# Moving splits, sums, a bias and a branch in a two-part graph network kernel

## The chip, the cores and the metric

The kernel runs on one core of a Trainium2 chip. A core has a matrix engine (TensorE, PE in the profile; its weight loads are listed as PEld), VectorE (DVE), ScalarE (ACT), GpSimd (POOL) and SyncE (SP), which here only issues transfers. Each engine works through its own queue of instructions in order and meets the others by semaphores. SBUF is the on-chip memory, PSUM the accumulators that TensorE writes, and DRAM is reached by DMA.

The metric is the device time of one execution in microseconds (us).

## The reference, cut to what matters

There are 1250 nodes with 1024 features, and 20000 edges sorted by their target. Two graph networks run one after the other, all in float32, each followed by a residual and a layer normalisation.

```
# first network
h = layernorm(x) * g + b
h = relu(h @ W1 + b1) @ W2 + b2              # 1024 -> 512 -> 256
for i in range(3):
    z = h + segment_sum(h[src], dst)
    z = relu(z @ Wa[i] + ba[i]) @ Wb[i] + bb[i]
    h = h + relu(layernorm(z) * ng[i] + nb[i])
delta = relu(h @ Wd1 + bd1) @ Wd2 + bd2      # 256 -> 512 -> 1024
x = layernorm(x + layernorm(x + delta) * og + ob)
# second network, two layers
deg_inv = 1 / max(in_degree, 1)
for l in range(2):
    mean = segment_sum(h[src], dst) * deg_inv
    h = h @ Wself[l] + mean @ Wneigh[l] + b[l]   # relu after the first
out = layernorm(x + h)
```

## The kernel before, in words

Every float32 product is made of three products of rounded halves: each operand is split into `hi` (rounded by ScalarE, `split_w` L123) and `lo = raw - hi` (a subtraction on VectorE or GpSimd), and `mm3` (L112) adds hi*hi, hi*lo and lo*hi in PSUM. So each weight costs one ScalarE pass and one subtraction.

**Encoder (0 to about 122 us).** Node rows are handled in tiles of 128 (ten tiles, pairs in `PCH`). A first block (L232 to L273) and a second (L502 to L554) are written in a fixed order by hand (`manual_schedule` over DVE, ACT, POOL and PE). They check the edge list, normalise and transpose the first x tiles, split W1 and run the first chunk of x @ W1. VectorE derives codes from the edge list in three steps (`codes(0..2)`, L278) that the one-hot matrices need.

The edges are summed into a dense adjacency matrix `A` (nodes by nodes, resident in SBUF). For each group of five edge tiles VectorE builds one-hot matrices R and Q (`one_hots`, L329), TensorE multiplies them into PSUM (`edge_tile`, L351), ScalarE copies a window of 50 columns into A at a place read from the integers `anci`, and GpSimd adds a carried column. This runs in between the encoder's products (`y_chunk`, `h_rows`), chunks 1 to 4.

The window scheme only works for edge lists that are dense enough. The first block counts whether this holds and leaves an integer `fli`: 0 for the fast way, 1 for the general one. `flag` (L389) is loaded from it on every engine, and `any_edges` (L390) holds a branch, `tc.If(flag > 0)`, around `general_adjacency`. It stands at the start of chunk 1. A second branch (L578) after the last edges reads A back. With these inputs neither body is entered; each engine has to compare and jump. `anci` is limited from above on VectorE (L264), so that the window stays inside A also for lists that take the general way.

After the last edges the unit matrix is added to A's diagonal (L577), so that A @ h is h + agg.

**Layers (about 122 to 262 us).** `load_wab(i)` (L611) loads and splits Wa[i] and Wb[i]; `begin_layer(i)` (L625) loads the layer's vectors. `agg(i, c, ..)` (L640) multiplies h by a block of A's columns and splits the result into `zh`, `zl`; `z1_chunk` (L657) and `z2_rows` (L670) are the two dense products, the normalisation and the new h rows. `asum` is the sum of A over its ten row blocks; the in-degrees come from it in `degrees` (L597, in layer 1). Rows 0 to 5 are summed ahead of the first `agg` (L744 to L746); rows 6 to 9 stand in layer 0's loop (L782 to L784) in two half widths. In the loop with i = 0, A is written to DRAM (`A_d`, L781), and W of layer 2 and the first two row blocks of the decoder's Wd2 are loaded; the third comes in layer 1 (L765). The branch for i = 1 (L789 to L791) loads Wd1, the last block of Wd2 and, by `load_bdo` (L710), the decoder's bias: four broadcast loads, six subtractions on VectorE and eight ScalarE passes, for three bfloat16 parts of bd2 - ob.

Layer weights, Wd1 and Wd2 are subtracted on GpSimd (`eng=G` in L611, `G` in L699 and L708). All of these loads, the layer's `bb` and the bias go through one ring of three buffers (`wraw`, L120), which also serves the second network. SP issues them in order; a load waits until the buffer's last user is done.

**Decoder and second network (262 us to the end).** The decoder's products, the second network with its seven half-size products per layer, and the output rows. The change touches nothing here.

Outside the hand-written blocks a planner in the framework fixes each engine's order when the program is built. It goes by the order in the source as priority, and by estimated durations and dependences: work that is late in the source can be put early in an engine's queue if the planner thinks the engine free, and a branch is one unit to it, with nothing of its body mixed with what is outside. On the chip the order is fixed.

Of the kernel before, what the change touches and what calls it, by code (L numbers as in the profile page):

```python
# [62 lines left out]

@with_exitstack
def tile_gnn(ctx, tc, x, es, vecs, W1, W2, b2, Wa, Wb, bb, ng, nb, Wd1, Wd2, bd2, og, ob,
             Ws0, Wn0, b0l, Ws1, Wn1, b1l, out):
# [101 lines left out]
    est = S1.tile([P, 2 * NGR * GT + 3 * (NGR + 1) + 3 * GT], I32, name="est")  # L168
    ne, o = NGR * GT, 2 * NGR * GT
    esrc, edst = est[:, :ne], est[:, ne:o].rearrange("p (g j) -> p g j", j=GT)  # L170
    anc, atop, agap = (est[:, o + i * (NGR + 1):o + (i + 1) * (NGR + 1)] for i in range(3))
    o += 3 * (NGR + 1)
# [59 lines left out]
    with tc.high_priority(), tc.manual_schedule(engines=order):  # L232
# [31 lines left out]
        V.tensor_tensor(anci, anc[0:1], atop[0:1], ALU.min)  # L264
# [6 lines left out]
        fli = S1.tile([1, 1], I32, name="fli")  # L271
        V.tensor_copy(fli, flf)
# [101 lines left out]
    def ahead(g):  # L374
        nonlocal n_oh
        while n_oh < min(NGR, g):
            one_hots(n_oh)
            n_oh += 1

    def some_edges(k):  # L380
        nonlocal n_ed
        for _ in range(k):
            ahead(n_ed // GT + LOOK + 1)
            if n_ed < ET:
                edge_tile(n_ed)
                n_ed += 1


    flag = nc.values_load(fli[0:1, 0:1], min_val=0, max_val=1)  # L389
    def any_edges():  # L390

        with tc.If(flag > 0):
            acc = Ap.tile([P, NT, AW], F32, name="acc", tag="A")
            V.memset(acc, 0.0)
            scratch = [B1.tile([P, 8 * (PW + 2)], F32, name=f"g{s}", tag=f"h0{s}0", bufs=1) for s in "hl"] + spare
            general_adjacency(tc, psp, acc[:, :, :N], (esrc, est[:, ne:2 * ne]), ident, ones, x, A_g, xg_d, scratch)
            res = Ap.tile([P, NT, AW], F32R, name="A", tag="A")
            nc.sync.dma_start(res.bitcast(F32)[:, :, :NN], A_g)
        return res
# [102 lines left out]
    with tc.manual_schedule(engines=order):  # L502
        std0 = bn_std(bn_mv(st0, 0))
        mv1 = bn_mv(bn(1), 1)

        parts = [bn_norm(0, *std0, ((0, HEAD), (HEAD, D)))]
        next(parts[0])
        parts.append(bn_norm(1, *bn_std(mv1), ((0, HEAD), (HEAD, D))))
        next(parts[1])
        split_W1(0, V)  # L510
        for part in parts:
            next(part)

        h0[0] = new_h0(0)
        for j in range(2):
            S.activation(h0[0][0][:, :, PW + j], vec[:, C_B:C_B + 8], AF.Copy)
            V.tensor_sub(h0[0][1][:, :, PW + j], vec[:, C_B:C_B + 8], h0[0][0][:, :, PW + j].bitcast(F32))
        transpose_x(0, (0,))
        split_W1(1)
        warm_up(WC)  # L520
        transpose_x(0, (2,))
        split_W1(2)
        mv2 = bn_mv(bn(2), 2)
        split_W1(3)
        std2 = bn_std(mv2)
        split_W1(4)
        next(bn_norm(2, *std2))
        codes(0)
        for f in range(4):
            first[f] = pst("ps_y", "ps" if f < 2 else "pa")  # L530
        for k in range(8):
            for f in range(4):
                fs = slice(f * P, f * P + P)
                mm3(first[f][:, :PW + 2], W1h[:, k, fs], W1l[:, k, fs], h0[0][0][:, k], h0[0][1][:, k],
                    k == 0, k == 7)
            if k == 0:
                transpose_x(0, (4,))
                split_W1(5)
                codes(1)
                mv3 = bn_mv(bn(3), 3)  # L540
            if k == 2:
                transpose_x(0, (6,))
                split_W1(6)
                std3 = bn_std(mv3)
                split_W1(7)
                next(bn_norm(3, *std3))
                codes(2)
            if k == 6:
                transpose_x(1, (0,))
        transpose_x(1, (2,))  # L550
        transpose_x(1, (4, 6))
        load_W2()
        V.tensor_copy(onesr, ones)
        ahead(2)  # L554
    for f in range(4):
        V.tensor_add(b1c[:, f:f + 1], first[f][:, PW:PW + 1], vec[:, C_B1 + f:C_B1 + f + 1])
    NC = len(PCH)
    SLOTS = 13
    for c in range(NC):
        if c == 1:  # L560
            A = any_edges()
        for f in range(4):
# [10 lines left out]
            if slot == SLOTS - 1:  # L573
# [4 lines left out]
                with tc.If(flag > 0):  # L578
                    nc.sync.dma_start(A.bitcast(F32)[:, :, :NN], A_g)
# [31 lines left out]
    def load_wab(i, eng=G):  # L611
# [81 lines left out]
    def load_Wd1():  # L693
        wd1h, wd1l = (B2.tile([P, 2, DH], F32R, name=f"wd1{s}", tag=f"w1{s}") for s in "hl")
        wd1.extend((wd1h, wd1l))
        for k in range(2):
            raw = wraw()
            nc.sync.dma_start(raw, Wd1[k * P:(k + 1) * P])
            split_w(raw, wd1h[:, k], wd1l[:, k], G)  # L699

    def load_Wd2(k):
        both = WD2.tile([P, 2, D], F32R, name=f"wd2_{k}", tag=f"wd2_{k}")
        hi, lo = wd2[k] = both[:, 0], both[:, 1]
        for i in range(2):
# [3 lines left out]
            split_w(raw, hi[:, fs], lo[:, fs], G)  # L708
# [35 lines left out]
    V.tensor_add(asum, A[:, 0, :NN].bitcast(F32), A[:, 1, :NN].bitcast(F32))  # L744
    for t in range(2, 6):
        V.tensor_add(asum[:gz(t)], asum[:gz(t)], A[:gz(t), t, :NN].bitcast(F32))  # L746
# [3 lines left out]
    for i in range(3):  # L750
# [12 lines left out]
        if i == 1:  # L763
            degrees()
            load_Wd2(2)  # L765
# [13 lines left out]
        if i == 0:  # L779
            with tc.issue_after(loads["nb"].ins):  # L780
                nc.sync.dma_start(A_d, A.bitcast(F32)[:, :, :NN])  # L781
            for t in range(6, NT):  # L782
                for cs in (slice(0, NN // 2), slice(NN // 2, NN)):
                    V.tensor_add(asum[:gz(t), cs], asum[:gz(t), cs], A[:gz(t), t, cs].bitcast(F32))  # L784
            load_wab(2)
            for k in range(2):
                load_Wd2(k)
        else:
            load_Wd1()  # L789
            load_Wd2(3)  # L790
            load_bdo()  # L791
# [877 lines left out]
```

## Time and profile before

| | |
|---|---|
| median of three runs | 923.88 us (922.95 to 924.91) |
| the profiled execution | 923.78 us, span 921.9 us |
| busy: PE, PEld | 894.7 us (97%), 788.2 us (85%) |
| busy: DVE, ACT, POOL | 645.0, 394.2, 87.7 us |
| mean granted TensorE clock | 0.99 |
| HBM read, written | 103.35 MB, 49.21 MB |

The span runs from the first to the last instruction; the device time is 1.9 us longer. Busy times overlap. A line such as `40.30 0.55 PE L113 MATMUL ps_h<-w2h,yh ... [4.00 <-PEq L392]` says: at 40.30 us TensorE began an instruction of line 113 that took 0.55 us, after 4.00 us idle that ended with its own sequencer at line 392. Line 113 to 115 are `mm3`, so tiles tell such lines apart. `PEclk` is the share of TensorE's full clock that was granted. Instructions of a queue's sequencer (`PEq`, `SPq`) do not count as busy time.

### The profile page before, as it was taken

To read this page: it belongs to the slowest core of one execution; us is meant where nothing else is said; L and a number is where in the kernel's file an instruction comes from. 1 tells how busy PE (TensorE), PEld (TensorE's weight loads), DVE (VectorE), ACT (ScalarE), POOL (GpSimd) and SP (SyncE) were. 2 spreads that over 40 slices of the span, in tenths; PEclk is the share of its full clock that TensorE was granted. 3 is DMA by queue.
4 is the path that set the end of the run, shared out by engine and by line. 5 is a ranking of instruction groups with operands and counts; after the bars stand their busy time and mean duration, and the time that the engine had idled before them with its cause. 6 is when DMAs were issued, how large, how long until landed. Compare 5 with 4: busy or idle time off the path is not lost.

```text
span 921.9 us, 13248 instructions
## 1 busy us (share of the span) xinstructions
PE 894.7 (97%) x4777; PEld 788.2 (85%) x4783; DVE 645.0 (70%) x1311; ACT 394.2 (43%) x760; POOL 87.7 (10%) x122
## 2 busy tenths in 40 slices
PE   7799998999899999999999999999999999999997
PEld 6799998988887778999988888889999888888885
DVE  8799678595976775565677675547466786777785
ACT  4577523454566873211133354543111333333454
POOL 4022234344201000000000000000000000000000
PEclk9799999999999999999999999999999999999999
DMA  7310058953115649997442236537895722322214
GB/s 243 118 42 2 1 197 217 312 177 103 61 52 202 224 145 348 336 310 254 170 148 72 77 127 197 172 125 264 287 306 214 235 80 77 85 72 76 81 47 177
DMA packets 83666, 148.35 MB, mean 161 GB/s; under 512 B 8296, under 2 KB 31995, under 8 KB 83082
## 3 DMA queue, kind: packets, MB, share of 16 engines
q1 hardware_dynamic: 77206, 126.90, 41.4%
q0 software_dynamic: 2176, 10.27, 4.5%
q10 hardware_dynamic: 4212, 10.27, 3.0%
q8 instruction: 38, 0.62, 0.3%
q14 instruction: 34, 0.28, 0.1%
HBM read 103.35 MB, written 49.21 MB: 165 GB/s over the span
## 4 chain that ended last, share of the span: by engine, by line
PE 83%; DVE 6%; DMA 4%; ACT 1%; issue 1%; POOL 0%; ACTq 0%; DVEq 0%; POOLq 0%; SPq 0%
PE ps_A L1222 20%; PE ps_m L113 14%; PE ps_m L115 14%; PE ps_m L114 14%; DMA wraw<-in_Wd_dram 3%; PE ps_dd L113 2%; PE ps_dd L115 2%; PE ps_dd L114 2%; PE pa L358 2%; PE ps_y L113 2%; PE ps_y L114 1%; PE ps_y L115 1%; PE ps_z L649 1%; DVE asum L746 1%; PE pt L974 1%
## 5 line engine op out<-in xcount | busy, mean ns | idle before, releaser
L113 PE MATMUL ps_m<-w,th 128*128 128x512 f32 x520 | 204.1, 392 | 0.0
L115 PE MATMUL ps_m<-w,th 128*128 128x512 f32 x520 | 202.6, 390 | 0.0
L114 PE MATMUL ps_m<-w,th 128*128 128x512 f32 x520 | 202.3, 389 | 0.0
L1222 PE MATMUL ps_A<-A,qh 128*128 128x418 f32 (+1 forms) x480 | 170.5, 355 | 0.0
L1222 PE MATMUL ps_A<-A,ql 128*128 128x418 f32 (+1 forms) x480 | 169.9, 354 | 0.0
L115 PEld LDWEIGHTS ps_m<-w,th 128*128 128x128 f32 x520 | 97.6, 188 | 20.7
L113 PEld LDWEIGHTS ps_m<-w,th 128*128 128x128 f32 x520 | 97.6, 188 | 19.8
L114 PEld LDWEIGHTS ps_m<-w,th 128*128 128x128 f32 x520 | 97.7, 188 | 19.7
L125 DVE TENSOR_TENSOR w<-stage,w 128x512 fp32r<-128x512 f32 x65 | 44.7, 690 | 68.2 <-ACT w L124 67.9
L1222 PEld LDWEIGHTS ps_A<-A,ql 128*128 128x128 f32 (+1 forms) x480 | 90.8, 189 | 1.9
L124 ACT ACTIVATE w<-stage 128x512 fp32r<-128x512 f32 x65 | 40.7, 629 | 118.8 <-PE ps_m L115 76.7
L1222 PEld LDWEIGHTS ps_A<-A,qh 128*128 128x128 f32 (+1 forms) x480 | 90.3, 188 | 1.2
L1227 DVE TENSOR_TENSOR MT<-ps_A,dgb 128x418 f32<-128x418 f32 x48 | 25.5, 586 | 64.6 <-PE ps_A L1222 64.6
L1183 ACT ACTIVATE qh<-qraw 128x1280 fp32r<-128x1280 f32 (+3 forms) x28 | 21.5, 809 | 105.1 <-PE ps_A L1222 102.8
L113 PE MATMUL ps_y<-h0h,w1h 128*128 128x256 f32 (+2 forms) x160 | 52.9, 331 | 0.0
L125 DVE TENSOR_TENSOR w<-wraw,w 128x512 fp32r<-128x512 f32 x39 | 26.9, 689 | 32.5 <-ACT w L124 30.7
L114 PE MATMUL ps_y<-h0l,w1h 128*128 128x256 f32 (+2 forms) x160 | 46.3, 289 | 2.9 <-DVE h0l L450 2.9
L1311 DVE TENSOR_TENSOR c<-ps_m,c 128x512 f32<-128x512 f32 (+1 forms) x65 | 40.9, 682 | 8.8 <-PE ps_m L115 8.7
L115 PE MATMUL ps_y<-h0h,w1l 128*128 128x256 f32 (+2 forms) x160 | 45.9, 287 | 0.0
L1052 ACT ACTIVATE th<-XT 128x640 fp32r<-128x640 f32 x48 | 34.2, 724 | 20.5 <-DVE MT L1227 20.5
L124 ACT ACTIVATE w<-wraw 128x512 fp32r<-128x512 f32 x39 | 24.5, 628 | 41.6 <-PE ps_m L115 21.3
L1053 DVE TENSOR_TENSOR th<-XT,th 128x640 fp32r<-128x640 f32 x48 | 39.5, 822 | 0.0
(307 smaller groups left out, 1842.4 us busy)
## 6 DMA issues: line engine op xcount, KB each, us to landing
A<-A_d SPq DMA_DIRECT2D x20, 627.0 KB
w_d<-stage SPq DMA_DIRECT2D x43, 256.0 KB
stage<-w_d SPq DMA_DIRECT2D x43, 256.0 KB
stage<-in_l_W_neigh_dram SPq DMA_DIRECT2D x42, 256.0 KB
stage<-in_l_W_self_dram SPq DMA_DIRECT2D x28, 256.0 KB
A_d<-A SPq DMA_DIRECT2D x1, 6270.0 KB
wraw<-in_l_W_neigh_dram SPq DMA_DIRECT2D x22, 256.0 KB
w_d<-wraw SPq DMA_DIRECT2D x21, 256.0 KB
```

Of the source, the lines that this page charges most:

```text
L113: T.matmul(ps, a_hi, b_hi, start=start, stop=False, skip_group_check=go_on)
L114: T.matmul(ps, a_hi, b_lo, start=False, stop=False, skip_group_check=go_on)
L115: T.matmul(ps, a_lo, b_hi, start=False, stop=stop, skip_group_check=go_on)
L124: S.activation(hi, raw, AF.Copy)
L125: return eng.tensor_sub(lo, raw, hi.bitcast(F32))
L358: T.matmul(pa[g][:, :, lo:hi], R[:, j], Q[j], start=j == 0, stop=end, skip_group_check=True)
L1052: S.activation(hi, src, AF.Copy)
L1053: V.tensor_sub(lo, src, hi.bitcast(F32))
L1183: S.activation(q[0][:, t0:t1], raw[:, t0:t1], AF.Copy)
L1222: T.matmul(pss[j][c][:, :w], qs[j][s][:n, t], A_of(t)[:n, c0:c0 + w], start=start and s == 0, stop=stop and s == 1)
L1227: V.tensor_mul(MT[:, f, c0:c0 + w], pss[j][c][:, :w], dgb[:, c0:c0 + w])
L1311: V.tensor_add(c, ps[:n], c if last or M in (6, 7) else c11[:n, t])
```

## The change

- The program body is now a function `gnn(..., fli, general, ...)` that is called twice: first the fast way, unconditionally; then `fli` is loaded and a branch holds a whole second copy, which computes everything again the general way. The two branches in the encoder and the flag's load there are gone. The copy without the general way has no `general_adjacency`.
- So that the fast copy stays inside A for every list, `anci` is now chosen between the true bases and even ones (a new row of constants in the index table): four one-partition operations on VectorE after `split_W1(2)` in place of one in the first block.
- `codes(0)`, `codes(1)` and `codes(2)` stand one place later each in the second block.
- `asum`: rows 1 to 4 (and 0) are added at the end of the encoder, in two half widths into a spare tile (eight operations); rows 5 to 9 ahead of the first `agg` (ten).
- The subtractions of layer weights, Wd1 and Wd2 go to VectorE: sixteen of 128 x 512.
- `load_bdo` and the third block of Wd2 move from layer 1's to layer 0's part of the loop, so they run beside layer 1 instead of layers 1 and 2.

```diff
+def tile_gnn(tc, *args):
+    with tc.tile_pool(name="keep", bufs=1) as keep:
+        fli = keep.tile([1, 1], I32, name="fli")
+        gnn(tc, fli, False, *args)
+        flag = tc.nc.values_load(fli, min_val=0, max_val=1)
+        with tc.If(flag > 0):
+            gnn(tc, None, True, *args)
+
 @with_exitstack
-def tile_gnn(ctx, tc, x, es, vecs, ...
+def gnn(ctx, tc, fli, general, x, es, vecs, ...
...
-    est = S1.tile([P, 2 * NGR * GT + 3 * (NGR + 1) + 3 * GT], I32, name="est")
+    est = S1.tile([P, 2 * NGR * GT + 4 * (NGR + 1) + 3 * GT], I32, name="est")
...
-        V.tensor_tensor(anci, anc[0:1], atop[0:1], ALU.min)
         warm_up(WA)
...
-        fli = S1.tile([1, 1], I32, name="fli")
-        V.tensor_copy(fli, flf)
+        if not general:
+            V.tensor_copy(fli, flf)
...
-    flag = nc.values_load(fli[0:1, 0:1], min_val=0, max_val=1)
     def any_edges():
-        with tc.If(flag > 0):
...
         split_W1(2)
+        V.tensor_tensor(acnt[:, 0:1], acnt[:, 0:1], acnt[:, 1:2], ALU.add)
+        V.tensor_scalar(acnt[:, 0:1], acnt[:, 0:1], 2 * NGR + 0.5, None, ALU.is_gt)
+        V.tensor_sub(ac, anc[0:1], even[0:1])
+        V.scalar_tensor_tensor(anci, ac, acnt[:, 0:1], even[0:1], ALU.mult, ALU.add)
         mv2 = bn_mv(bn(2), 2)
...
         next(bn_norm(2, *std2))
-        codes(0)
...
             if k == 0:
                 transpose_x(0, (4,))
                 split_W1(5)
-                codes(1)
+                codes(0)
                 mv3 = bn_mv(bn(3), 3)
...
                 next(bn_norm(3, *std3))
-                codes(2)
+                codes(1)
...
         V.tensor_copy(onesr, ones)
+        codes(2)
         ahead(2)
...
+    HALVES = (slice(0, NN // 2), slice(NN // 2, NN))
+    EARLY = 4
...
         if c == 1:
-            A = any_edges()
+            A = any_edges() if general else Ap.tile([P, NT, AW], F32R, name="A", tag="A")
...
-                with tc.If(flag > 0):
-                    nc.sync.dma_start(A.bitcast(F32)[:, :, :NN], A_g)
+            if slot == SLOTS - 1:
+                sums = [spare[0][:, cs] for cs in HALVES]
+                for t in range(1, EARLY + 1):
+                    for half, cs in zip(sums, HALVES):
+                        V.tensor_add(half, A[:, 0, cs].bitcast(F32) if t == 1 else half, A[:, t, cs].bitcast(F32))
...
-    def load_wab(i, eng=G):
+    def load_wab(i, eng=V):
...
-            split_w(raw, wd1h[:, k], wd1l[:, k], G)
+            split_w(raw, wd1h[:, k], wd1l[:, k], V)
...
-            split_w(raw, hi[:, fs], lo[:, fs], G)
+            split_w(raw, hi[:, fs], lo[:, fs], V)
...
-    V.tensor_add(asum, A[:, 0, :NN].bitcast(F32), A[:, 1, :NN].bitcast(F32))
-    for t in range(2, 6):
-        V.tensor_add(asum[:gz(t)], asum[:gz(t)], A[:gz(t), t, :NN].bitcast(F32))
+    for t in range(EARLY + 1, NT):
+        for half, cs in zip(sums, HALVES):
+            V.tensor_add(asum[:gz(t), cs], (half if t == EARLY + 1 else asum[:, cs])[:gz(t)],
+                         A[:gz(t), t, cs].bitcast(F32))
...
             degrees()
-            load_Wd2(2)
...
-            for t in range(6, NT):
-                for cs in (slice(0, NN // 2), slice(NN // 2, NN)):
-                    V.tensor_add(asum[:gz(t), cs], asum[:gz(t), cs], A[:gz(t), t, cs].bitcast(F32))
             load_wab(2)
-            for k in range(2):
+            load_bdo()
+            for k in range(3):
                 load_Wd2(k)
         else:
             load_Wd1()
             load_Wd2(3)
-            load_bdo()
...
+    evens = [g * 40 for g in range(NGR)] + [NN]
```

More of the change, by code (lines that the diff above doesn't have):

```diff
@@ L61, in rz, with gnn @@
     return P if t < NT - 1 else N - (NT - 1) * P
+def tile_gnn(tc, *args):
[5 more added lines that the diff above has]
+            gnn(tc, None, True, *args)
 @with_exitstack
-def tile_gnn(ctx, tc, x, es, vecs, W1, W2, b2, Wa, Wb, bb, ng, nb, Wd1, Wd2, bd2, og, ob,
-             Ws0, Wn0, b0l, Ws1, Wn1, b1l, out):
+def gnn(ctx, tc, fli, general, x, es, vecs, W1, W2, b2, Wa, Wb, bb, ng, nb, Wd1, Wd2, bd2, og, ob,
+        Ws0, Wn0, b0l, Ws1, Wn1, b1l, out):
     nc = tc.nc
@@ L166, in tile_gnn @@
     epsc0 = S1.tile([P, 1], F32, name="epsc0")
-    est = S1.tile([P, 2 * NGR * GT + 3 * (NGR + 1) + 3 * GT], I32, name="est")
+    est = S1.tile([P, 2 * NGR * GT + 4 * (NGR + 1) + 3 * GT], I32, name="est")
     ne, o = NGR * GT, 2 * NGR * GT
     esrc, edst = est[:, :ne], est[:, ne:o].rearrange("p (g j) -> p g j", j=GT)
-    anc, atop, agap = (est[:, o + i * (NGR + 1):o + (i + 1) * (NGR + 1)] for i in range(3))
-    o += 3 * (NGR + 1)
+    anc, atop, agap, even = (est[:, o + i * (NGR + 1):o + (i + 1) * (NGR + 1)] for i in range(4))
+    o += 4 * (NGR + 1)
     woff, wwid, wend = (est[:, o + i * GT:o + (i + 1) * GT].unsqueeze(1).broadcast_to([P, NGR, GT])
@@ L375, in ahead @@
         nonlocal n_oh
-        while n_oh < min(NGR, g):
+        while n_oh < min(NGR, g) and not general:
             one_hots(n_oh)
@@ L383, in some_edges @@
             ahead(n_ed // GT + LOOK + 1)
-            if n_ed < ET:
+            if n_ed < ET and not general:
                 edge_tile(n_ed)
                 n_ed += 1
-    flag = nc.values_load(fli[0:1, 0:1], min_val=0, max_val=1)
     def any_edges():
[L392 to L398, printed above, removed]
+        acc = Ap.tile([P, NT, AW], F32, name="acc", tag="A")
+        V.memset(acc, 0.0)
+        scratch = [B1.tile([P, 8 * (PW + 2)], F32, name=f"g{s}", tag=f"h0{s}0", bufs=1) for s in "hl"] + spare
+        general_adjacency(tc, psp, acc[:, :, :N], (esrc, est[:, ne:2 * ne]), ident, ones, x, A_g, xg_d, scratch)
+        res = Ap.tile([P, NT, AW], F32R, name="A", tag="A")
+        nc.sync.dma_start(res.bitcast(F32)[:, :, :NN], A_g)
         return res
@@ L572, in tile_gnn @@
                     ln_x(2 * c + 3 + f)
-            if slot == SLOTS - 1:
+            if slot == SLOTS - 1 and not general:
                 for t in range(NT):
@@ L1642 @@
     gaps = [GW] * (NGR - 1) + [GWL, 0]
+    evens = [g * 40 for g in range(NGR)] + [NN]
     wins = [lo for lo, _ in WIN] + [hi - lo for lo, hi in WIN] + [0] * (GT - 1) + [1]
-    consts = np.broadcast_to(np.concatenate([bases, tops, gaps, wins]).astype(a["dst"].dtype), (P, 3 * (NGR + 1 + GT)))
+    consts = np.broadcast_to(np.concatenate([bases, tops, gaps, evens, wins]).astype(a["dst"].dtype), (P, 4 * (NGR + 1) + 3 * GT))
     es = np.ascontiguousarray(np.concatenate([edges(a["src"], 0), edges(a["dst"], -1), consts], axis=1))
```

## The prediction

> **What bounds the kernel now.** I read the page's busy shares and the slices first. TensorE is busy for 97% of the span and from 345 us on without a break, so time can only be won or lost ahead of that, or after the last matmul.
>
> ```profile
> PE 894.7 (97%) x4777; PEld 788.2 (85%) x4783; DVE 645.0 (70%) x1311; ACT 394.2 (43%) x760; POOL 87.7 (10%) x122
> PE   7799998999899999999999999999999999999997
> PEclk9799999999999999999999999999999999999999
> ```
>
> Next the table by stretches (start:end, length, busy time of PE, PEld, DVE, ACT, POOL, granted clock) around the dips: TensorE pays twice, first idle, then at half clock.
>
> ```profile
> 36.00:38.00 2.00, 0.31 (x3) 0.10 (x1) 0.68 (x3) 1.04 (x2) 0.00 (x0) 1.00 0.78 248
> 38.00:40.00 2.00, 0.00 (x0) 0.00 (x0) 2.00 (x10) 0.00 (x0) 0.00 (x0) 0.85 0.00 0
> 40.00:42.00 2.00, 1.70 (x8) 1.52 (x9) 1.18 (x5) 0.00 (x0) 0.00 (x0) 0.50 0.03 8
> 42.00:44.00 2.00, 2.00 (x12) 1.83 (x11) 0.49 (x1) 0.66 (x2) 0.00 (x0) 0.50 0.01 4
> 44.00:46.00 2.00, 1.79 (x10) 1.36 (x9) 0.03 (x1) 1.97 (x5) 0.21 (x1) 0.50 0.00 0
> ```
>
> Then the timeline (start, length, work, and in brackets the idle time before it and what ended it) at the three gaps, and the instructions of line 392, the edge branch:
>
> ```profile
> L392 SPq EVENT_SEMAPHORE  x8: 17/17/17, 36.2 to 39.1; - x8
> L392 PEldq COMPARE_BRANCH  x1: 3858/3858/3858, 36.3 to 36.3; - x1
> ...
> 40.30 0.55 PE L113 MATMUL ps_h<-w2h,yh 128*128 128x256 f32 x1 [4.00 <-PEq L392]
> ...
> 135.45 5.87 DVE L784 TENSOR_TENSOR asum<-asum,A 128x627 f32<-128x627 f32 x8
> 141.23 1.01 DVE L655 TENSOR_TENSOR zl<-ps_z,zh 128x384 fp32r<-128x384 f32 x2
> ...
> 141.83 0.69 PE L114 MATMUL ps_z<-zl,wabh 128*128 128x384 f32 x1 [3.17 <-DVE zl L655]
> ...
> 229.29 0.70 DVE L720 TENSOR_TENSOR wraw<-wraw 128x512 f32<-128x512 f32 x1 [1.59 <-issue]
> ...
> 231.96 0.39 PE L113 MATMUL ps_z<-wabh,z1h 128*128 128x256 f32 x1 [1.73 <-ACT z1h L152]
> ```
>
> The reader is to see three owners: the branch itself (TensorE's jump took 3.86 us); in-degree sums that VectorE runs ahead of the `zl` that TensorE needs; and the decoder bias, which sits in VectorE's and ScalarE's queues ahead of `z1h` in layer 2. Last, the chain of waits and POOL in layer 1, where the bias now goes:
>
> ```profile
> 174.79 21.23 DMA wraw<-in_Wd_dram
> ...
> 198.77 4.13 POOL L125 TENSOR_TENSOR wd<-wraw,wd 128x512 fp32r<-128x512 f32 x3
> ```
>
> A decoder weight asked for at 174.79 lands at 196.0, behind the 6.27 MB write of `A_d` issued at 172.18.
>
> **Part by part** (minus is gain; times of the profiled execution, 923.78 us: span 921.9 and 1.9 around it, 0.1 under the median).
>
> 1. Middle branch (L392, L578 and the flag's load) gone. On TensorE it costs 4.00 idle and then half of the 5.49 busy between 40 and 46, 2.7: at most 6.7. VectorE worked through the gap, so it may not follow: to 50 us it is idle 1.33 (its own jump), 1.33, 2.96 and 0.33, so at most 6.0 can be taken out of its row, and surely the 1.33. ScalarE's copy of the first edge group (42.87) needs the group's one-hots, which VectorE would end near 36.5; the product after that allows it about 37.3, 5.6 earlier. I take -5.0, nearest to the ScalarE and VectorE rows; ends -6.7 and -1.3. L578 is 0.2 on TensorE with no idle after it: nothing.
>
> 2. Start. `anci` leaves the first VectorE chain, and four operations of one partition (0.14 to 0.2 each, rows at 5.08 to 11.48) come in before the statistics of x tile 2: +0.7, of which 0.77 of VectorE's idle ahead of 16.16 (ScalarE waits there for W1 anyway) covers most. `codes(0)`, 1.33 + 1.44, now follows the `h0l` that TensorE waited 2.0 for at 18.9; that wait goes, but the next `h0l` pair (now 23.96) then stands behind it and bn(3), 1.28, and is ready near 23.3, when TensorE would want it near 21.6. So the wait moves on by two blocks. VectorE is busy almost without a pause to 36, so the stage's end hardly moves: 0; ends -1.6 (the slow stretch 22.3 to 25.6) and +0.7. The longer index table is 33 more integers a row, under 0.1.
>
> 3. Eight half-width sums at the end of the encoder, 5.87/8 = 0.73 each, 5.9 in all. VectorE is 2.0 busy of the 8 us from 112 to 120, so they fit; but in its queue they stand ahead of the last `yl` pairs, wanted by `ps_h` from 118.9: +0.5, ends 0 and +1.5.
>
> 4. Start of layer 0. VectorE's sums there took 1.46 + 9.59 + 1.45 + 5.87 = 18.4 (one of them 5.6, beside POOL subtractions, against 1.45). Now ten halves, 7.3; four weight splits come from POOL, 4 x 0.69 = 2.8; bias split and cast 0.6; POOL's two remaining subtractions may hold it up for 1.5. From 122.5 that ends by 134.7; the first `zh` is done at 136.4, so `zl` follows at once. The gap, 3.17, goes, and its slow clock: 141.83 to 145.2 holds 10.5 products at 0.32 instead of 0.175, 1.5. -4.7; ends -4.7 and 0 (VectorE 3 us later than I count). What hides the splits here is the aggregation on TensorE, 121.95 to 138.3. Behind VectorE's splits SP's next ring load waits as it did behind POOL's.
>
> 5. Bias out of layer 2: 1.73 + 0.35 idle, and from 233.9 to 237.4 the slow clock: ten products at 0.30 for 0.165 and three at 0.21 for 0.12, 1.6. -3.7; at least -2.1. Without it `z1h` would follow `ysp` near 229.5, before TensorE is done at 230.2. Next late is `z1l` of the second half, about 230.7, wanted at 230.8.
>
> 6. Layer 1 takes the bias (six VectorE subtractions of 0.69 = 4.1, eight ScalarE passes of 0.63 = 5.0, four loads) and six Wd2 splits on VectorE, 4.1, with two loads more. POOL's versions stretched VectorE's own work between 198 and 208 (1.36, 1.32, 1.40 and 0.89 for rows of 0.42 to 0.48: about 3.6), so VectorE gains 4.6 net. It has 1.8 idle between 196 and 216 and rows 7 to 9 have 3 us in hand before TensorE wants them at 220.2. TensorE already idles 2.3 there (200 to 212). SP's queue: the second bias load waits for a ring buffer held until the first bias is through (6.4 us in the row from 225.0 to 231.4), and behind it stand Wd2, the degrees' transfers, `bb` of layer 2 and Wd1. These move from about 197 to 206 and later, `bb` near 220 for use near 233, Wd1 near 225 for use at 252: hidden by layer 1's aggregation. POOL loses 10.5 + 9.0 + 2.5 = 22.0 us of work, and its `h1l` come sooner. +1.0; ends -2.3 (today's gaps close) and +6.4 (all 4.6 on the path, and 1.6 to 1.8 of slow clock). Wd1 and Wd2(3), four splits, fall in 216 to 222, where VectorE is idle: 0.
>
> 7. End. The flag is loaded (0.47 on SP) and every engine jumps over a second copy of the program. TensorE (done 915.2), VectorE and ScalarE (918.7) have time. SP issues its last store until 919.15 and today waits for it until 921.1, 1.95. For the middle branch, branch to next instruction was 0.5 on SP, 0.8 POOL, 1.2 ACT, 2.9 DVE, 3.9 TensorE; SP jumped over few instructions there, now over several hundred, so I take the two long rows: 0.47 + 2.9 to 3.9 less 1.95 = 1.4 to 2.4. +2.0; ends 0 (SP's own row) and +5.4 (3 us more, as its eight semaphore steps took from 36.2 to 39.1).
>
> Sum: -5.0 + 0 + 0.5 - 4.7 - 3.7 + 1.0 + 2.0 = -9.9, so 923.78 - 9.9 = 913.9.
>
> [...] Gaps of 1.73, 2.0, 3.17 and 4.00 were each followed by 3.3 to 6 us at a granted clock of 0.5; gaps of 1.1 (at 31) and 1.2 (at 201.4) were not. [...]
>
> **Rivals.**
> A. VectorE sets the encoder's pace: it is 22.2 and 22.0 busy of 23 in the two stretches from 46 to 92. Then only its 1.33 comes back, 3.7 less: 917.6. Against it: 4.6 of idle before 50.
> B. Layer 1 takes the bias's price in full, +6.4 for +1.0: 919.3. For it: VectorE is 95% busy from 188 to 204; against it: its idle 6.6 us at 216 to 222.
> C. Slower. VectorE's queue is in order. If the planner places the first bias subtraction ahead of layer 1's `zl` (178.23), VectorE stands until the load lands at 196, and TensorE, out of work near 182, until about 198: 16 + 1.6 for the clock, in place of the 1.0: 930.5. It decides once that stall passes 12.8. Against it: ScalarE's matching Wd2 step today waited only 0.89 for its load, so the planner knows of the write.
> D. Several covers fail at once, or the planner, no longer split by the branch, orders the encoder worse than I can see: about 922 to 928.
>
> **Numbers.** Forecast 0.57, A 0.17, B 0.14, C 0.08, D 0.04. All best ends together give -19 (905), which needs every one; the range 908 to 921 holds the forecast with one or two terms at their ends, A and B, and leaves out C and D and some of the tails. For the sign, 0.2% is about what a measurement of this kernel can tell from no change: 1.85 us, 922.0 to 925.7. A, B and the forecast lie under it; with tails: faster 0.86, same 0.03, slower 0.11.
>
> **What the changed profile would show.** Right: no gap with a branch as its releaser near 36; no 3 us gap between the aggregation and `z1` of layer 0; none near 230; `wab`, `wd1`, `wd` splits on DVE at 0.69; bias subtractions in layer 1 after the A_d write; SP's compare-branch after the last store, with about 3 us to the next instruction. Wrong: a gap of TensorE over 2 us in layer 1 with a bias or Wd2 load behind it; the 36 to 46 us stretch still at clock 0.5; or a tail over 5 us longer.

## The result, and the profile after

The changed kernel takes 917.33 us (median of four runs, 915.28 to 917.94) where the kernel before takes 924.39 (922.95 to 926.03): 0.9929 of the time, interval 0.9915 to 0.9943. It is faster by 7 us. The prediction was 913.9, range 908 to 921.

The profiled execution took 917.94 us, span 916.1; the one of before 923.78, span 921.9. Its page, busy shares and slices:

```profile
PE 891.3 (97%) x4783; PEld 783.0 (85%) x4783; DVE 649.6 (71%) x1335; ACT 393.0 (43%) x760; POOL 79.2 (9%) x106
PE   7899999999999999999999999999999999999995
PEclk8999999999999999999999999999999999999998
```

A slice is 23 us. The dips of before in the seventh and eleventh (138 to 161 and 230 to 253 us) are gone, and the second, with the branch's gap, is better. New are a lower clock in the first slice and in the last, and less work in the last one, since the end behind the last product is longer.

To see where the time went, I set one VectorE operation at the end of each stage beside the same operation of before. The difference of two such rows, less the difference at the end of the stage ahead, is what the stage alone gained (minus) or lost. A second profile of the changed kernel (the first experiment) stands beside it, since the spans of the two differ by 3.2 us.

| stage, and the operation at its end | before, us | after | second profile | stage alone: after | second | on record |
|---|---|---|---|---|---|---|
| start: first `b1c` | 27.85 | 30.11 | 28.12 | +2.26 | +0.27 | 0 (part 2) |
| encoder: first unit matrix added to A | 109.26 | 108.04 | 104.54 | -3.48 | -4.99 | -5.0 (part 1) |
| its end: last `hf` | 122.15 | 121.33 | 117.83 | +0.40 | +0.40 | +0.5 (part 3) |
| layer 0: first `zl` of layer 1 | 178.23 | 172.32 | 168.82 | -5.09 | -5.09 | -4.7 (part 4) |
| layer 1: third `zl` of layer 2 | 225.62 | 219.65 | 215.90 | -0.06 | -0.31 | +1.0 (part 6) |
| layer 2: last `z1l` | 252.87 | 244.13 | 240.67 | -2.77 | -2.48 | -3.7 (part 5) |
| rest: last `c<-ps_m` on VectorE | 915.36 | 906.43 | 903.15 | -0.19 | -0.01 | 0 |
| tail: end of the span | 921.9 | 916.1 | 912.9 | +3.1 | +3.2 | +2.0 (part 7) |
| sum | | | | -5.8 | -9.0 | -9.9 |

**The encoder after.** The table by stretches (start:end, length, busy time of PE, PEld, DVE, ACT, POOL, clock) of the changed kernel, where before TensorE stood for 4.00 us and then ran at 0.50:

```profile
36.00:40.00 4.00, 3.39 (x24) 2.55 (x24) 4.00 (x16) 2.14 (x7) 0.00 (x0) 1.00 0.51 178
40.00:44.00 4.00, 2.53 (x14) 1.50 (x13) 3.98 (x15) 3.92 (x10) 0.22 (x1) 1.00 0.01 2
44.00:48.00 4.00, 3.81 (x21) 3.63 (x22) 4.00 (x14) 3.38 (x10) 2.49 (x3) 0.61 0.00 0
```

The gap is gone, and VectorE (third pair of numbers) is now busy for 12 of 12 us: it sets the pace here. TensorE waits in six small gaps, none over 0.65, and falls to half clock in the stretch at 44 all the same (0.50 from 45 to 48).

**The layers after**, timeline (start, length, work, and the idle time before it with what ended it):

```profile
135.56 0.56 DVE L673 TENSOR_TENSOR zl<-ps_z,zh 128x384 fp32r<-128x384 f32 x1 [3.18 <-ACT zh L672]
...
195.51 0.69 DVE L738 TENSOR_TENSOR wraw<-wraw 128x512 f32<-128x512 f32 x1 [1.31 <-DMA wraw<-in_out_b_dram]
...
197.03 0.51 DVE L673 TENSOR_TENSOR zl<-ps_z,zh 128x358 fp32r<-128x358 f32 x1
...
197.60 0.43 PE L124 MATMUL ps_z<-zl,wabh 128*128 128x358 f32 x1 [1.21 <-DVE zl L673]
...
208.44 0.38 PE L125 MATMUL ps_z<-wabh,z1l 128*128 128x256 f32 x1 [0.75 <-DVE z1l L165]
...
241.54 0.39 PE L124 MATMUL ps_d<-hT,wd1h 128*128 128x256 f32 x1 [0.76 <-DVE hT L833]
```

In layer 0 VectorE now waits 3.18 us for ScalarE's `zh`, where before TensorE waited 3.17 us for VectorE's `zl`. In layer 2 the only gap of TensorE over 0.3 us is the 0.76 at `hT`. In layer 1 VectorE stands 1.31 us at a bias subtraction whose load has not landed, with `zl` behind it in the queue, and TensorE pays 1.21 for it.

**The end after**, the instructions of line 70, the branch around the second copy (durations in ns, then first and last start):

```profile
L70 SPq EVENT_SEMAPHORE  x8: 17/17/17, 913.4 to 914.0; - x8
...
L70 PEldq COMPARE_BRANCH  x1: 3662/3662/3662, 902.8 to 902.8; - x1
...
L70 ACTq COMPARE_BRANCH  x1: 50/50/50, 909.5 to 909.5; - x1
L70 SPq COMPARE_BRANCH  x1: 53/53/53, 910.3 to 910.3; - x1
L70 ACTq EVENT_SEMAPHORE  x1: 17/17/17, 912.4 to 912.4; - x1
```

From SP's branch to its next instruction it is 3.1 us (910.3 to 913.4), on ScalarE 2.9. TensorE's jump, 3.66 from 902.8, was over at 906.5, while TensorE's last products still ran until 906.4. The last work of ScalarE, in this profile (span 916.1) and in the one of before (span 921.9):

```profile
908.97 0.81 ACT L1283 ACTIVATE c<-c,nb__9319,rs 128x512 f32<-128x512 f32 x1 [0.48 <-DVE nb__9319 L1278]
...
917.89 0.81 ACT L1268 ACTIVATE c<-c,nb__10065,rs 128x512 f32<-128x512 f32 x1 [0.48 <-DVE nb__10065 L1263]
```

Behind it come 6.3 us, where before there were 3.2.

### The profile page after: what moved, and what is told of

Same layout as the page of the kernel before. It is cut to its first block, busy times and chain, and to the rows that moved or that the text cites. A ratio compares the mean times of both kernels' runs of the same rounds, so it can differ in the third digit from the quotient of the medians.

```text
span 916.1 us, 13254 instructions
## 1 busy us (share of the span) xinstructions
PE 891.3 (97%) x4783; PEld 783.0 (85%) x4783; DVE 649.6 (71%) x1335; ACT 393.0 (43%) x760; POOL 79.2 (9%) x106
## 4 chain that ended last, share of the span: by engine, by line
PE 84%; DVE 8%; issue 3%; ACT 2%; DMA 1%; POOL 0%; POOLq 0%; ACTq 0%; DVEq 0%
PE ps_A L1237 20%; PE ps_m L123 14%; PE ps_m L125 14%; PE ps_m L124 14%; PE ps_z L667 4%; PE ps_dd L123 2%; PE ps_dd L125 2%; PE ps_dd L124 2%; PE pa L367 1%; PE ps_y L123 1%; PE pt L989 1%; PE pt L1258 1%; PE ps_y L124 1%; PE ps_y L125 1%; PE ps_z L124 1%
```

## The experiments

Each was timed in five rounds beside the kernel before, on one chip per group. Ratios are to the kernel before in the same group.

### The changed kernel again

No edit.

> The changed kernel once more, to see whether its start is its own. In its first profile the second x tile was late: VectorE waited 1.31 us for it and took its statistics at 8.13 us (before: 6.98), TensorE ran at half clock until 14 us, and the first bias column of the encoder (b1c) came at 30.11 against 27.85, 2.26 later. Theory 'chance of the transfer': the tile lands earlier this time, statistics near 7.0, b1c near 28, and the profiled execution is 1 to 2 us shorter than 917.9. Rival 'the change's own' (the longer index table or the order of the transfers): statistics again near 8.1, b1c near 30.1. Either way 0.993 of the time before.

Measured: 914.93 us, ratio 0.9911 (0.9894 to 0.9929). The start of the first profile and of this one, timeline:

```profile
8.13 1.29 DVE L213 BATCH_NORM_STATS2 st<-xs 128x6 f32<-128x512 f32 x2 [1.31 <-DMA xs<-in_x_dram]
...
10.23 0.45 PE L452 MATMUL pt<-ident,xs 128*128 128x128 f32 x1 [4.07 <-issue]
```

```profile
6.55 1.23 DVE L213 BATCH_NORM_STATS2 st<-xs 128x6 f32<-128x512 f32 x2
...
8.60 0.30 PE L452 MATMUL pt<-ident,xs 128*128 128x128 f32 x1 [1.83 <-issue]
```

The same program took the statistics of its second x tile 1.6 us sooner, without a wait, and had `b1c` at 28.12 for 30.11. So 2.0 of the 2.26 us were this execution's, not the change's; that not all of the late start was, the third experiment shows. The stretches after 40 us differ too (this second profile):

```profile
40.00:44.00 4.00, 2.82 (x23) 2.03 (x23) 3.98 (x15) 4.00 (x11) 0.48 (x2) 1.00 0.01 2
44.00:48.00 4.00, 4.00 (x37) 3.76 (x36) 4.00 (x15) 2.74 (x11) 2.99 (x5) 1.00 0.00 0
```

With the same small gaps the clock stayed at 1.00 this time. With it go the 1.5 us between -3.48 and -4.99 in the ledger. Over the six profiles with this start, the half clock at 44 came three times (the first, and the runs without the tail and with the bias back: -3.5 in that stage each) and stayed away three times (this one, and the runs with GpSimd's subtractions and with the old sums: -5.0 each).

### Without the end's branch

```diff
-        flag = tc.nc.values_load(fli, min_val=0, max_val=1)
-        with tc.If(flag > 0):
-            gnn(tc, None, True, *args)
```

> The changed kernel without the branch and the second copy at the end; the general way is left out. Theory 'the jump over the copy lengthens the tail': from ScalarE's last operation to the end of the span goes from 6.3 us back to about 3.2, as before, so 3.1 less: about 914.2, 0.9895 of the time before. By the term on record (+2.0): 915.3. Rival 'the end waits for the last store anyway': 917.3, unchanged.

The kernel leaves out the general way. Measured: 912.14 us, 0.9873 (0.9854 to 0.9893), 2.8 us under the changed kernel's median in the same group (3.5 by the ratios). From the end of ScalarE's last operation (907.01) to the end of the span (910.3) it is 3.3 us, in the changed kernel 6.3 (909.78 to 916.1), in the kernel before 3.2. The copy at the end costs 2.8 to 3.5 us, not 2.0.

### Only the branches taken out

```diff
-    flag = nc.values_load(fli[0:1, 0:1], min_val=0, max_val=1)
...
-        with tc.If(flag > 0):
-            acc = Ap.tile([P, NT, AW], F32, name="acc", tag="A")
...
-            nc.sync.dma_start(res.bitcast(F32)[:, :, :NN], A_g)
...
-                with tc.If(flag > 0):
-                    nc.sync.dma_start(A.bitcast(F32)[:, :, :NN], A_g)
```

> The kernel before, with its two branches in the encoder, their bodies and the flag's load taken out and nothing else (the general way is left out). The term on record says 5.0 less: about 919.4, 0.9946 of the time before. Rival 'VectorE sets the encoder's pace': only its own 1.33 comes back, 923.1, 0.9986. The changed kernel's profile stands between: its encoder ends 1.2 us earlier although it started 2.26 later, which would be 3.5 less: 920.9, 0.9962. In the profile: no 4.0 us gap near 36 to 40 and, by the theory, TensorE not below 3.7 of 4 us busy in 36 to 48; by the rival gaps that VectorE's one-hots and yl end, 2 us or more of them.

This kernel too leaves out the general way. Measured: 920.97 us, 0.9969 (0.9955 to 0.9983). In its profile, the shortest of its seven executions (919.32), the encoder from `b1c` to the unit matrix is 5.35 shorter than before: part 1's size, in a profile. The ratio of the medians says 2.9 (1.6 to 4.2), less than the 5.0, more than the rival's 1.3.

Part of the difference lies ahead of `b1c`, in a term that the record doesn't have. `pw` are warm-up products, whose results nothing uses; `pt` are the transposes of x. TensorE's timeline of before, and of this run:

```profile
5.60 1.37 PE L227 MATMUL pw<-iq 128*128 128x256 f16 x11
9.03 0.30 PE L445 MATMUL pt<-ident,xs 128*128 128x128 f32 x1 [2.05 <-issue]
...
10.11 0.82 PE L227 MATMUL pw<-iq 128*128 128x256 f16 x6
11.50 0.66 PE L445 MATMUL pt<-ident,xs 128*128 128x128 f32 x4 [0.58 <-DVE flf L270]
```

```profile
5.75 0.39 PE L227 MATMUL pw<-iq 128*128 128x256 f16 x2
9.63 0.45 PE L439 MATMUL pt<-ident,xs 128*128 128x128 f32 x1 [3.49 <-issue]
...
11.22 2.40 PE L227 MATMUL pw<-iq 128*128 128x256 f16 x15
13.46 0.60 PE L439 MATMUL pt<-ident,xs 128*128 128x128 f32 x4
```

With the branch in the encoder, eleven of these products stand ahead of the first transpose and six in the block behind the fourth; so it is in all three profiles that have this branch (before, and two runs below). In the eleven profiles without it two to four stand ahead and thirteen to fifteen behind. In these eleven the clock falls to 0.50 for 3.3 us or more between 7 and 15 us, in the three it stays at 1.00; the second block of four transposes follows later, and `b1c` comes at 28.12 to 30.11 us (mean 29.1) against 27.70 to 28.02. So the start gives back about 1.2 us, and of the 5.35 about 4.1 is left, which the interval holds. That the moved products are the cause is read from these rows; no run changed their order alone.

### The old start

```diff
+        V.tensor_tensor(anci, anc[0:1], atop[0:1], ALU.min)
         warm_up(WA)
...
         split_W1(2)
-        V.tensor_tensor(acnt[:, 0:1], acnt[:, 0:1], acnt[:, 1:2], ALU.add)
-        V.tensor_scalar(acnt[:, 0:1], acnt[:, 0:1], 2 * NGR + 0.5, None, ALU.is_gt)
-        V.tensor_sub(ac, anc[0:1], even[0:1])
-        V.scalar_tensor_tensor(anci, ac, acnt[:, 0:1], even[0:1], ALU.mult, ALU.add)
...
+        codes(0)
         for f in range(4):
...
-                codes(0)
+                codes(1)
...
-                codes(1)
+                codes(2)
...
-        codes(2)
         ahead(2)
```

> The changed kernel with the start as it was: one operation for anci in the first block, the three steps of codes each one place earlier. Theory 'VectorE's chain': the four one-partition operations took 2.6 us and not 0.7, and codes(2) fell into 36.5 to 37.5, where VectorE is busy 16.0 of 16 us (32 to 48) and TensorE waits for its yl and Q; undone, the encoder ends about 2 us earlier: 915.3, 0.9907 of the time before. Rival 'hidden', the term on record (0): 917.3, 0.993.

Measured: 913.83 us, 0.9890 (0.9873 to 0.9908): 1.1 us under the changed kernel, but the intervals overlap. The profile, by stretches:

```profile
36.00:40.00 4.00, 3.85 (x29) 3.03 (x28) 4.00 (x17) 3.32 (x10) 0.00 (x0) 1.00 0.40 135
40.00:44.00 4.00, 3.37 (x25) 2.60 (x24) 3.39 (x12) 3.26 (x8) 0.54 (x2) 1.00 0.01 2
44.00:48.00 4.00, 3.65 (x32) 3.24 (x31) 3.85 (x10) 3.31 (x10) 1.93 (x3) 1.00 0.00 0
```

VectorE has air again, TensorE is 3.37 busy instead of 2.5 to 2.8 in 40 to 44, and the stage is -5.37. It was -5.35 to -5.38 in all five profiles without the branch and with the old start (this one, the run above, and three below): with the old order the slow stretch never came.

### The bias back in the second pass

```diff
             load_wab(2)
-            load_bdo()
...
             load_Wd2(3)
+            load_bdo()
```

> The changed kernel with the bias loaded where it was, in the second pass of the loop, behind Wd1 and the last block of Wd2; the three Wd2 blocks stay in the first pass. Two profiles of the changed kernel gain 2.8 us from the middle of layer 1 to the end of layer 2. Theory of the record (layer 2 without the bias -3.7, layer 1 with bias and splits +1.0): with the bias back layer 2 pays 2.1 to 3.7 again, and layer 1, without its six subtractions, gets back at most 1: 2 to 3 us slower than the changed kernel's 914.9, about 917.5, 0.994 of the time before. Rival B (layer 1 takes the bias's price in full): 914.9, 0.991. In the profile: a gap of TensorE of 1 to 2 us in layer 2 ended by z1h or z1l, with bias subtractions ahead of it on VectorE.

Measured: 918.45 us, 0.9934 (0.9922 to 0.9947): 0.0023 or 2.1 us over the changed kernel's 0.9911. Timeline of TensorE and VectorE in layer 2:

```profile
223.95 0.38 PE L123 MATMUL ps_z<-wabh,z1h 128*128 128x256 f32 x1 [0.81 <-DVE z1h L164]
...
225.35 0.69 DVE L738 TENSOR_TENSOR wraw<-wraw 128x512 f32<-128x512 f32 x1 [0.86 <-DMA wraw<-in_out_b_dram]
...
229.41 0.39 PE L125 MATMUL ps_z<-wabh,z1l 128*128 128x256 f32 x1 [0.77 <-DVE z1l L165]
```

The gaps are back, 0.81 and 0.77, and no half clock behind them (mean clock 1.00 from 220 to 260 us). The theory of the record holds; rival B does not. With the splits on VectorE the old place of the bias costs 2.1, less than the 3.7 read from the kernel before, where the slow clock followed its gap of 1.73.

### The subtractions back on GpSimd

```diff
-    def load_wab(i, eng=V):
+    def load_wab(i, eng=G):
...
-            split_w(raw, wd1h[:, k], wd1l[:, k], V)
+            split_w(raw, wd1h[:, k], wd1l[:, k], G)
...
-            split_w(raw, hi[:, fs], lo[:, fs], V)
+            split_w(raw, hi[:, fs], lo[:, fs], G)
```

> The changed kernel with the sixteen weight subtractions (layer weights, Wd1, Wd2) on GpSimd again. Theory of the record: GpSimd's subtractions stretch VectorE's operations beside them (rows of 0.45 us took 0.9 to 1.4, a sum of 1.45 took 5.6), so the sums ahead of zl in layer 0 end later and part of the 3.2 us gap comes back, and VectorE gains little in layer 1: 1 to 3 us slower than 914.9, about 917, 0.993 of the time before. Rival 'VectorE is the fuller engine' (95% busy from 188 to 204): 16 x 0.69 = 11 us off VectorE make layer 1 up to 2 us faster: 913, 0.989. Third: all of it is hidden, 914.9.

Measured: 926.26 us, 1.0020 (1.0008 to 1.0031). All the rest of the change, without this part, is slower than the kernel before, and 10 us slower than the whole change. None of the theories had that. Timeline:

```profile
118.97 7.02 POOL L135 TENSOR_TENSOR wabl<-wraw,wabh 128x512 fp32r<-128x512 f32 x1 [0.18 <-ACT wabh L134]
...
144.54 0.51 PE L697 MATMUL ps_z<-bbc,onesr 128*128 128x256 f32 x2 [2.93 <-DMA bbc<-wraw]
...
198.85 0.69 DVE L738 TENSOR_TENSOR wraw<-wraw 128x512 f32<-128x512 f32 x1 [5.04 <-DMA wraw<-in_out_b_dram]
...
200.11 0.40 PE L123 MATMUL ps_z<-zh,wabh 128*128 128x358 f32 x1 [2.75 <-DVE asum L620]
```

A subtraction that takes GpSimd 1.29 us elsewhere took 7.02, until 126.0, beside VectorE's sums (half-width ones, which took the usual 0.7 each). It holds a ring buffer: SP's load of Wb, which waits for it, goes out at 126.01, 7.5 us after the encoder's last `hf` (1.9 in the changed kernel). The loads of `bb` follow it in the queue, and what TensorE needs at 141.6 lands 2.9 us late. In layer 1 the bias is late the same way: VectorE stands 5.04 us with everything behind it, and TensorE idles 2.75 and 2.11 us and runs at a mean clock of 0.83 from 200 to 220. That is rival C's mechanism. The gap ahead of `zl` in layer 0 stayed away all the same: between the last `hf` and the first `zl` this run gains 4.8 us, as the changed kernel does.

### The old sums

```diff
-                sums = [spare[0][:, cs] for cs in HALVES]
-                for t in range(1, EARLY + 1):
...
-    for t in range(EARLY + 1, NT):
...
+    V.tensor_add(asum, A[:, 0, :NN].bitcast(F32), A[:, 1, :NN].bitcast(F32))
+    for t in range(2, 6):
+        V.tensor_add(asum[:gz(t)], asum[:gz(t)], A[:gz(t), t, :NN].bitcast(F32))
...
+            for t in range(6, NT):
+                for cs in (slice(0, NN // 2), slice(NN // 2, NN)):
+                    V.tensor_add(asum[:gz(t), cs], asum[:gz(t), cs], A[:gz(t), t, cs].bitcast(F32))
             load_wab(2)
```

> The changed kernel with the sums of A's rows as they were: none at the end of the encoder, rows 0 to 5 ahead of the first aggregation, rows 6 to 9 in the loop of layer 0. Theory of the record (+0.5 at the encoder's end, -4.7 in layer 0): 4.2 us slower than 914.9, about 919.1, 0.9957 of the time before, with a gap of TensorE of about 3 us ended by zl near 135 to 140 and half clock after it. Rival 'the gap went because the weight splits left GpSimd, whose subtractions stretched one sum to 5.6 us': the gap stays away or under 1 us, 915 to 916.

Measured: 916.56 us, 0.9914 (0.9900 to 0.9927): no difference from the changed kernel. The 0.40 at the encoder's end is gone, and layer 0 is still 5.1 faster. VectorE's timeline ahead of `zl`:

```profile
118.44 1.46 DVE L756 TENSOR_TENSOR asum<-A 128x1254 f32<-128x1254 f32 x1
119.81 1.89 DVE L135 TENSOR_TENSOR wabl<-wraw,wabh 128x512 fp32r<-128x512 f32 x3
121.62 3.38 DVE L758 TENSOR_TENSOR asum<-asum,A 128x1254 f32<-128x1254 f32 x2
...
132.46 0.55 DVE L667 TENSOR_TENSOR zl<-ps_z,zh 128x384 fp32r<-128x384 f32 x1
```

Two full-width sums take 3.38 with the splits in VectorE's own queue; in the kernel before three took 9.59 beside GpSimd's subtractions. The rival holds: the sums need not be cut or begun early. In this profile layer 1 is 0.6 longer than before, where in the changed kernel it was 0.1 to 0.3 shorter; the times don't show it.

### More warm-up at the start

```diff
-    WA, WB, WC = 20, 16, 4
+    WA, WB, WC = 20, 28, 4
```

This is on top of the old start.

> The changed kernel with the old start (as in the run of that name, 913.8) and twelve more warm-up products in the first block (28 for 16), so that TensorE is at work until about 8.3 us. In five of six profiles TensorE went to half clock for 3.3 to 6 us between 7 and 15 us, after 1.8 to 4.1 us without a product; only the profile of the kernel before did not. Theory 'the idle time sets off the half clock': the clock holds until 15 us, the first bias column comes near 28 in every profile, and the time is 1 to 2 us less: 912.3, 0.9875 of the time before. Rival 'the start waits for x and VectorE anyway, the slow products are hidden': 913.8, 0.989. Slower (914.5) if the products stand in the way of the first transposes.

Measured: 915.77 us, 0.9911 (0.9895 to 0.9926), no gain. The profile shows TensorE idle from 6.1 to 8.9 us as before, at half clock (0.50) from 8 to 14.6, and VectorE waiting behind the extra products:

```profile
16.03 0.87 DVE L458 SCALAR_TENSOR_TENSOR h0l<-pt,vec,h0h 128x256 fp32r<-128x256 f32 x2 [3.54 <-PE pw L237]
```

The products did not fill the hole: TensorE's queue has all twelve after the first transpose. So this run doesn't tell what a full clock at the start is worth, and the question stays open.

### Only the splits

The diff of the GpSimd run the other way round, on the kernel before: `G` to `V` in three places.

> The kernel before, with nothing changed but the engine of the sixteen weight subtractions (VectorE for GpSimd). In the run with the old sums the gap ahead of zl in layer 0 stayed away, in the run with GpSimd's subtractions too; so by the theory 'either change alone is enough' the gap of 3.17 us and its slow clock go here: about 5.0 less, 919.0, 0.9946 of the time before; the gap in layer 2 (bias) stays. By the run with GpSimd's subtractions (11 us slower than the changed kernel) the engine could be worth more than that also here, up to 11: that took the bias and the third Wd2 block in layer 1's queue, which are not there, so at most 2 more: 917. Rival 'the splits only help together with the smaller sums': 924, unchanged, the gap at 141 is there.

Measured: 919.47 us, 0.9944 (0.9930 to 0.9958), as expected. TensorE's gaps at the branch and in layer 2:

```profile
40.72 0.55 PE L113 MATMUL ps_h<-w2h,yh 128*128 128x256 f32 x1 [4.57 <-PEq L392]
46.22 0.33 PE L445 MATMUL pt<-ident,xs 128*128 128x128 f32 x1 [1.11 <-ACT xs L146]
...
227.24 0.38 PE L113 MATMUL ps_z<-wabh,z1h 128*128 128x256 f32 x1 [0.81 <-DVE z1h L154]
232.81 0.38 PE L115 MATMUL ps_z<-wabh,z1l 128*128 128x256 f32 x1 [0.78 <-DVE z1l L155]
```

In its profile layer 0 alone is 4.3 faster (first `zl` of layer 1 at 174.36 for 178.23, with the last `hf` 0.43 later), and 5.0 at its own fifth `zl`. Three letters are two thirds of the whole change. The first two lines show something else. Behind the branch's gap the clock was at 1.00 again from 44 us, where before it had a mean of 0.72 from 44 to 48, and still the first `hf` came no earlier (48.22 for 47.98): TensorE then waited 1.11 for ScalarE.

### Old start and old sums together

The two diffs above on the changed kernel.

> The changed kernel with the old start and the old sums together. Old sums spare the 0.4 us at the encoder's end and cost nothing in layer 0, the old start was 1.1 us better: about 1 us under the changed kernel's 0.9911, 0.990, about 914.8 where before is 924. Rival 'the old sums in the loop collide with the bias's load in layer 1': the changed kernel's time or 1 more.

Measured: 916.33 us, 0.9902 (0.9887 to 0.9918). The ratio is the first theory's 0.990, though the interval holds the changed kernel's too. In the profile the rival is at work as well: layer 1, taken from its third `zl` to the third of layer 2, is 3.0 us longer than in the kernel before (0.04 shorter in the changed kernel), with a gap of 2.12 us at `zh` and a clock of 0.78 from 190 to 200.

### Wd2's third block later

```diff
             load_bdo()
-            for k in range(3):
+            for k in range(2):
...
             load_Wd1()
+            load_Wd2(2)
             load_Wd2(3)
```

This is on top of the last run.

> As the run with the old start and old sums, and Wd2's third block loaded and split in the second pass, behind Wd1. TensorE's idle time in layer 1 (about 1.4 us from 200 to 220 us, 0.75 of it ended by a z1l that stood behind Wd2's subtractions on VectorE) should fall by the 0.7, for a split that moves to where VectorE has 6 us free: 0.5 to 1 us less than that run, 0.989. Rival 'layer 1's idle time is that of the bias load and its ring, not of the splits': no difference. Slower by up to 1 if Wd1 and the third block now crowd layer 2.

Measured: 914.59 us, 0.9888 (0.9871 to 0.9904), the lowest ratio of all complete kernels. Layer 1 is 1.0 longer than before in its profile, 2.0 less than in the last run. It beats the kernel before; from the changed kernel's 0.9911 and from the last run it isn't separated.

### The branch in the middle again

The last run's kernel with the branches of before and no copy at the end (the kernel before, plus splits on VectorE, bias and Wd2 blocks moved).

> The kernel before with the splits on VectorE and the bias loaded in the first pass of the loop, Wd2's third block behind Wd1 in the second: the last run's kernel, but with the two branches in the encoder as before and no second copy at the end. Taking the branches out alone gave 0.9969, taking the copy at the end away gave 0.9873 for 0.9911. Theory 'moving the branch wins in the encoder what it costs at the end': no difference from the last run, 0.9888, within 0.001. By the record (-5.0 + 2.0): 3.0 us slower than it, 0.992.

Measured: 921.61 us, 0.9970 (0.9961 to 0.9980). Both expectations were wrong: by the ratios it is 7.6 us slower than the run above, not 0 or 3.0. The two profiles differ by 5.4: 4.6 in the encoder (5.9 behind `b1c`, less 1.3 ahead of it, where this run has the products' order of before), 0.9 in layer 0 to its end at the third `zl` of layer 1, 2.1 in layer 1, 1.0 behind it, and -3.2 in the tail. Layer 1 of this run, and of the run above:

```profile
195.95 0.69 DVE L720 TENSOR_TENSOR wraw<-wraw 128x512 f32<-128x512 f32 x1 [2.04 <-DMA wraw<-in_out_b_dram]
...
200.06 0.59 PE L113 MATMUL ps_z<-zh,wabh 128*128 128x358 f32 x2 [2.11 <-ACT zh L654]
201.85 0.67 PE L114 MATMUL ps_z<-zl,wabh 128*128 128x358 f32 x1 [1.03 <-DVE zl L655]
```

```profile
193.56 0.60 PE L123 MATMUL ps_z<-zh,wabh 128*128 128x358 f32 x2 [1.12 <-ACT zh L663]
195.49 0.67 PE L124 MATMUL ps_z<-zl,wabh 128*128 128x358 f32 x1 [1.17 <-DVE zl L664]
```

The bias's load made VectorE wait 2.04 and 1.12 us here, 1.06 and 1.26 there. TensorE's two gaps are 3.14 here and 2.29 there, and behind them the mean clock was 0.66 from 200 to 210 us here, 0.83 from 195 to 205 there. Why the load lands later with the branch in the encoder, and what the 0.9 in layer 0 and the 1.0 behind layer 1 are, stays open. So it is not settled what moving the branch is worth by itself: taking it out alone wins 2.9 and the copy costs 2.8 to 3.5 at the end, together nothing, but here the kernel with the branch in the middle was far behind. Nor is the bias's new place a gain by itself: this run is 2.4 us slower by the ratios than the run with only the splits, which has the bias (and Wd2's third block) in the old place, while in the changed kernel the new place won 2.1.

## Why the prediction was right, and where its steps were not

The sign and the range held. The second profile follows the sum closely (-9.0 for -9.9); the medians, 917.33 and 914.93 in two groups, lie 3.4 and 1.0 us above 913.9. That the sum comes so near is in part luck: in the second profile the cost in layer 1 had been put 1.3 too high, the gain in layer 2 1.2 too high, and the cost of the end 1.2 too low.

1. **Middle branch, -5.0.** Right in size behind `b1c`: -5.35 with the old start. With the 1.2 that the start gives back it is about 4.1, and 4.6 in the last pair. Two things under it were wrong. The slow clock behind the gap (2.7 in my upper end) was hardly on the path: in the run with only the splits it ended sooner, the gap ended 0.4 later than before, and the first `hf` came 0.2 later. And rival A's mechanism, VectorE as the pace, is real from 36 to 48 us, with the change's later `codes`: -5.0 where the clock stayed at 1.00 behind the small gaps, -3.5 where it fell to 0.50.
2. **Start, 0.** Mis-sized. The four one-partition operations took 1.07, 0.14, 1.18 and 0.24 us, 2.6 and not the 0.7 from rows of 0.14 to 0.2, and `codes(2)` landed at 36.5 where VectorE has no air. The old start is 1.1 better between medians with overlapping intervals; only the profiles' encoder stage (-5.37 against -4.99 and -3.48) shows it. What the step overlooked is TensorE's own queue: without the branch most warm-up products stand behind the first transposes, and `b1c` is later by 1.2 on average, 0.27 to 2.26 by the execution.
3. **Encoder's end, +0.5.** Measured 0.40, and 0.0 with the old sums.
4. **Layer 0, -4.7.** Measured -5.1. The step gave the gain to fewer sums and to splits off GpSimd together. The runs separate them: splits alone are enough, and so are the smaller sums alone for the `zl` gap, but with a GpSimd subtraction stretched to 7.02 us the ring is late, and in that run layer 0 ended 1.8 slower than before, not 5.1 faster.
5. **Layer 2, -3.7.** Measured -2.5 and -2.8, and 2.1 when the bias went back. The slow clock was priced about right, 1.6: in the run with only the branches out the old gaps (1.68 and 0.35) stood with the clock at 1.00 behind them, and layer 2 was 1.50 shorter. What the sum left out is TensorE's gap at `hT` in layer 2, which is not in the profile of before: 0.76 and 0.72 in the two profiles. It was 0.47 in five others with the bias in the new place (without the tail, and the old start, old sums, both, and more warm-up), and there the stage gained 3.4.
6. **Layer 1, +1.0.** Measured -0.1 to -0.3. Rival B fell. Rival C was real but small: VectorE did stand for the bias's load ahead of a `zl`, but the planner put the first subtraction at 191.4 and only the second was late, 1.31, so TensorE lost 1.21 and not 16. How near it was the GpSimd run shows: 5.04.
7. **End, +2.0.** Measured +3.1. From SP's branch to its next instruction it is 3.1, within the 2.9 to 3.9 that I took, and the flag's load was free, since SP made it at 29.0 us. What I left out are the eight semaphore steps (913.4 to 914.0), another 0.8 us on SP (914.0 to 914.8), and a final meeting of the engines that takes 1.3 us (914.8 to 916.1) instead of 0.8 (921.1 to 921.9).

Parts 5 and 6 together (-2.7) came out at -2.8 in both profiles, the error of one covering that of the other.

The slow clock was priced from the gaps of one profile, and the length of a gap does not tell in these profiles whether it comes. It came three times in six behind one and the same pattern of small gaps. A gap of 1.83 us at the start (second profile) and a stretch with 1.5 us idle in 4 were followed by half clock, while gaps of 2.05 in the profile of before, 1.98 in the run with only the splits (1.00 in all its stretches but 40 to 44) and 1.68 in the run with only the branches out (1.00 from 220 to 260) left the clock at 1.00. What sets it off was not shown.

The jumps over the second copy took 3.7 us on TensorE, 3.1 on VectorE and SP, 3.0 on GpSimd and 2.9 on ScalarE. Over the middle branch the short rows were 0.5 on SP, 0.8 on GpSimd and 1.2 on ScalarE, so the two long ones, 2.9 and 3.9, were the ones to take.

## What to carry to other kernels

Before pricing a wait, look at which engine runs beside it: a row measured while VectorE and GpSimd work at the same time may not be the operation's own cost (three sums 9.59 us beside GpSimd's subtractions, two 3.38 without them), and moving the subtractions to the queue of the fuller engine won here (0.9944 by itself). Judge a change made of several edits by taking the edits out one at a time: here three letters carried two thirds of it, one part (the sums) carried nothing that the times show, and the rest without the splits was slower than no change. The jump over the copy took 2.9 to 3.7 us on every engine here, and it was free only where other work ran beside it (TensorE's from 902.8, GpSimd's from 548.0). And look at the order that the planner gives the whole program after an edit: taking the branch out moved TensorE's products 25 us ahead of it.

## What was not expected of the hardware

- Executions of one program on one chip differ by 3.5 us (921.87 to 925.38 for the kernel before in the first group). Two profiles of the changed kernel place most of their 3.2 us in the first 50: the statistics of the second x tile began at 6.55 and 8.13 us, and the half clock at 44 came once. A single profile's ledger of a start is worth about 2 us either way.
- No long gap stood ahead of the half clock at 44: six gaps of at most 0.66 us, with 1.2 to 1.5 us idle in 4, were followed by it in three of six profiles (mean clock from 44 to 48 us 0.61, 0.68 and 0.57; 1.00 in the other three).
- VectorE's sums and GpSimd's subtractions took two to five times as long beside each other: three sums of 1254 columns took 9.59 us beside GpSimd's subtractions (one of them 5.6) and about 1.5 to 1.7 each without them; of the subtractions, 1.29 each elsewhere, one took 2.62 there, and one 7.02 in the run that put them back on GpSimd, beside half-width sums that kept their usual 0.7.
- TensorE's jump over the second copy, 3.66 us, cost nothing: it lay beside its own last products (902.8 to 906.5, the products until 906.4).
